# Gated linear attention and a 4-bit MLP on one core: other home counts, the key factors behind the chunk's step, and identity matmuls at the start

## The chip, the cores and the metric

The kernel runs on one core of one Trainium2 chip. The metric is the device time of the whole program in microseconds (us); the time before is the median of three runs. TensorE is called PE, its weight loads PEld, VectorE DVE, ScalarE ACT, GpSimd POOL and SyncE, which issues nearly all transfers, SP.

## The reference

Two residual blocks follow each other, on x of 4 batches x 512 tokens x 512 features, all in 32-bit floats:

```python
x = x + attention(layernorm(x))        # 4 heads of 128, chunks of 128 tokens
x = x + mlp(layernorm(x))              # 512 -> 4096 -> 512
```

The attention is gated and linear. From the normed x come q, k, v (512 wide each), and for each head a gate alpha = sigmoid(...) and a weight beta = softplus(...). k is divided by its norm over each head. In each chunk, with cla the running sum of log(alpha):

```python
attn   = (q @ k.T) * beta.T * tril(exp(cla - cla.T))
y      = attn @ v + exp(cla) * (q @ state)
state  = state * exp(cla_end) + v.T @ (k * beta * exp(cla_end - cla))
```

The MLP's weights come as 4-bit codes, two to a byte in an integer, with a scale for each block of 32:

```python
inter = gelu_tanh(x @ Wg.T) * (x @ Wu.T)     # 2048 tokens x 4096
out   = inter @ Wd.T
```

## The kernel before

**Stages.** The attention phase fills about the first 300 us, the MLP overlaps its last 70 us and runs to the end. Attention goes over 4 batches b; each batch has twelve steps, counted through by p: j = 0 to 3 make v and the gates' inputs for one tile of 128 tokens (`product_v`, PE lines 381 and 388), j = 4 to 7 make one head of q (`product_q`, L406), j = 8 to 11 one tile of k (`product_k`, L418). After each step stands `behind(p)`, which adds what lies behind that product: for the chunk number (p - 9) // 3 it is, in turn for p % 3 = 0, 1, 2, the lead (k transposed at L520, copied by ACT to kT at L523), the values (kw and vb, POOL L569 and L573) and the decay (ACT's exponentials L536, POOL's causal mask L540, qc and the state's decay); then the scores (PE L581, DVE L589); then the sums (PE L600 to L611, DVE adds y to the residual tile xr at L616, stores it at L617, starts the second layernorm, and updates the state at L620 or L622).

**Norms.** A layernorm has three parts. `norm` issues statistics (DVE L310, L312, POOL L314, L315); `settle` writes the normed tile hn (DVE L320); `turn("a")` (first norm) or `turn("f")` (second) transposes it on PE (L341) and copies it out: for the first norm ACT writes hT (L351), for the second ACT and DVE split it into three parts g (L362 to L364), which SP stores to DRAM (h2, L366). For the MLP they are loaded again as x (L296), twelve tiles of 128x512 for a batch.

**MLP.** A round i takes one batch (i % 4) through up to four blocks of 128 of the 4096 columns. For each block `gate_up` makes two products (pa eight matmuls, pb four, L696), with the elementwise work at L701 to L718; each product's value stands in a tile called t. `down` then multiplies into eight PSUM banks (p_d, L734) and adds to the accumulator tiles acc (DVE L747 and L748), which are stored (L749) and loaded again four rounds later. There are 35 rounds. The x tiles of the next round are loaded in two parts: the first six during this round, the rest after this round's last product (`load_x`). The 4-bit weights are unpacked by DVE and ACT one piece at a time (`unpack`, `fetch`), ahead of their use.

**Order.** The whole order of each engine is written out by hand: the program is issued in source order under a manual schedule, each engine works through its own list, and semaphores hold an instruction back until its inputs are there and its buffers are free.

**Homes.** Nearly all on-chip tiles live in slots called homes, of 4 KB a partition (`two_k`) or 2 KB (`one_k`). The free ones are a list: `get` takes the home that was given back longest ago, `put` appends. When no small home is free, `get` takes a large one whole. A new tile in a home waits for the last reader of the tile that was in it before, a store to DRAM among them. PSUM has eight banks, handed round in turn.

**The start.** SP issues the loads in order, ACT issues four small ones (Wab, bab, bv, bq) and then an exponential on a dummy value (`warm`, which loads the table). `first(n)` is norm and settle of tile n; the copy of Wab into the joint weight tile is POOL's L833. During batch 0 `product_v` calls `between` between its two products: turn("a"), and the norm of the tile after next.

Of the kernel before, what the change touches and what calls it, by code (L numbers as in the profile page):

```python
# [21 lines left out]
P = 128  # L22
# [13 lines left out]
def f32(t):  # L36
    return t.bitcast(F32)
# [3 lines left out]
def tile_gated_linear_attention__then__nvfp4_geglu(  # L41
# [19 lines left out]
    nc = tc.nc  # L61
    B, T, D = x.shape
    H = D // P
    NCH = T // P
# [52 lines left out]
                else:  # L117
                    self.free.append(tag)

    two_k = Homes("a", 24, [P, 2, T])  # L120
    one_k = Homes("b", 42, [P, T], two_k)

    def psum(name):
        return fps.tile([P, T], F32, tag="p", name=name)

    def heads(t):
        return t.rearrange("p (h d) -> p h d", d=P)
# [5 lines left out]
    ident = const.tile([P, P], F32, tag="ident", name="ident")  # L133
# [160 lines left out]
    def load(src, name):  # L294
        t = one_k.get(name)
        nc.sync.dma_start(f32(t), src)  # L296
        return t

    def tile_of(t):
        return xf[t * P : (t + 1) * P, :]  # L300

    def rows(src, c):
        return src.rearrange("(c p two) n -> c p two n", p=P, two=2)[c]
# [26 lines left out]
    def settle():  # L330
        for then in settled:
            then()
        settled.clear()
# [80 lines left out]
    def product_k(b, n):  # L414

        pk = psum(f"pk_{b}_{n}")
        for k in range(KC):
            nc.tensor.matmul(  # L418
                pk, f32(hT[b][k // 2])[:, k % 2, n * P : (n + 1) * P], f32(wk[k // 2])[:, k % 2, :],
                start=(k == 0), stop=(k == KC - 1),  # L420
            )
        kt = one_k.get(f"k_{b}_{n}")
        k_sb[b, n] = kt
        nc.vector.tensor_tensor(f32(kt), pk, f32(bk_sb), ALU.add)
        sq = one_k.get(f"sq_{b}_{n}")
        nc.scalar.activation(f32(sq), f32(kt), AF.Square)
        sn = small.tile([P, H], F32, tag="ss", name=f"ss{b}_{n}")
        nc.vector.tensor_reduce(sn, heads(f32(sq)), AX.X, ALU.add)
        one_k.put(sq)
        nc.gpsimd.tensor_scalar(sn, sn, 1e-24, None, ALU.max)  # L430
        nc.gpsimd.tensor_tensor(sn, sn, minus_half, ALU.pow)
        brn = small.tile([P, H], F32, tag="brn", name=f"brn{b}_{n}")
        nc.gpsimd.tensor_tensor(brn, sn, beta[b][:, n * H : (n + 1) * H], ALU.mult)
        kwf = small.tile([P, H], F32, tag="kwf", name=f"kwf{b}_{n}")
        nc.gpsimd.tensor_tensor(kwf, sn, bdte[b][:, n * H : (n + 1) * H], ALU.mult)
        ss[b, n] = brn, kwf
# [189 lines left out]
    for b in range(1, B):  # L626
        for n in range(NCH):
            p = 3 * NCH * (b - 1) + 3 * n - 1 if b > 1 else 2 + 3 * min(n, 2)
# [50 lines left out]
    jk = [(j, k) for j in range(3) for k in range(KC)]  # L679
    x3 = [[] for _ in rounds]  # L680

    def load_x(i, which):
        if i < len(rounds):
            for j, k in which:
                x3[i].append(load(h2d[i % B][j][k], f"x_{i}_{j}_{k}"))
# [73 lines left out]
    def mlp():  # L759
        for i, r in enumerate(rounds):  # L760
            ts = range(i % B * NCH, (i % B + 1) * NCH)
            ms = tiles[i]
            inter = []
            a4 = residual(i) if i > 1 else None
            ahead = [0] if i >= B - 1 else [i] if i > 0 else []
            for q, mt in enumerate(ms):
                if q in ahead:
                    load_x(i + 1, jk[:6])

                def last():  # L770

                    if q == len(ms) - 1:
                        one_k.put(*x3[i])
                        if i == 1:
                            nonlocal a4
                            a4 = residual(i)
                        load_x(i + 1, jk[len(x3[i + 1]) :] if i + 1 < len(rounds) else [])

                inter.append((yield from gate_up(mt, x3[i], 2 if i == 1 else 1, r + MC, last, f"{i}_{mt}", mt == ms[-1] and len(ms) < 3)))
                if mt == r and mt < tiles[-1][0]:  # L780
                    two_k.put(*wgu[mt])
            final = i + B >= len(rounds)
            dst = [of[t * P : (t + 1) * P, :] if final else accd[t] for t in ts]
            if i == 0:
                over = ms, inter
                continue
            if i == B:
                ms, inter = over[0] + ms, over[1] + inter
            down(ms, inter, a4, dst, f"{i}", i == len(rounds) - 1)
            if r >= 0 and r % 2 == 1 and r < tiles[-1][0]:  # L790
                two_k.put(*wd[r // 2])
            yield


    with tc.manual_schedule():
        wab_sb = const.tile([P, KC, 2 * H], F32, tag="wab", name="wab_sb")
        bq_sb = const.tile([P, H], F32, tag="bq", name="bq_sb")
        bab_sb = const.tile([P, 2 * H], F32, tag="bab", name="bab_sb")
        bv_sb, bk_sb = one_k.get("bv"), one_k.get("bk")
        wva = [two_k.get(f"wva{c}") for c in range(KC // 2)]  # L800
        wvb = two_k.get("wvb")
        wvb_ = f32(wvb).rearrange("p two (k n) -> p (two k) n", n=VB + 2 * H)
        wq, wk = ([two_k.get(f"w{nm}{c}") for c in range(KC // 2)] for nm in "qk")
        x0 = [load(tile_of(0), "x0_0")]
        nc.scalar.dma_start(
            wab_sb.rearrange("p (c two) n -> p c two n", two=2),
            Wab.rearrange("(c p two) n -> p c two n", p=P, two=2),
        )
        nc.scalar.dma_start(bab_sb, bab.partition_broadcast(P))
        nc.scalar.dma_start(f32(bv_sb), bv.partition_broadcast(P))  # L810
        nc.scalar.dma_start(bq_sb, bqT)

        warm = small.tile([P, 1], F32, tag="warm", name="warm")
        nc.scalar.activation(warm, eps_la, AF.Exp)
        for c in range(KC // 2):
            nc.sync.dma_start(f32(wva[c])[:, :, :VA], rows(Wv, c)[:, :, :VA])
        x0.append(load(tile_of(1), "x0_1"))
        for c in range(KC // 2):
            nc.sync.dma_start(wvb_[:, 2 * c : 2 * c + 2, :VB], rows(Wv, c)[:, :, VA:])
        x0 += [load(tile_of(n), f"x0_{n}") for n in range(2, NCH)]  # L820
        for w, src in ((wq, Wq), (wk, Wk)):
            for c in range(KC // 2):
                nc.sync.dma_start(f32(w[c]), rows(src, c))
        nc.sync.dma_start(f32(bk_sb), bk.partition_broadcast(P))
        for n in range(NCH):
            xs[1, n] = load(tile_of(NCH + n), f"x1_{n}")

        def first(n):
            first_norm(0, n, x0[n])
            settle()  # L830

        first(0)
        nc.gpsimd.tensor_copy(wvb_[:, :, VB:], wab_sb)  # L833
        constants()
        turn("a")
        first(1)
        blocks = mlp()
        p = 0
        for b in range(B):
            for j in range(3 * NCH):  # L840
                if j < NCH:
                    if b == 0:

                        def between():
                            turn("a")
                            if j + 2 < NCH:
                                first(j + 2)

                        product_v(b, j, between)
                    else:  # L850
                        product_v(b, j)
                elif j < 2 * NCH:
                    product_q(b, j - NCH)
                else:
                    product_k(b, j - 2 * NCH)
                if b == B - 1:
                    if j == NCH - 1:
                        two_k.put(*wva, wvb)
                        one_k.put(bv_sb)
                    elif j == 2 * NCH - 1:  # L860
                        two_k.put(*wq)
                    elif j == 3 * NCH - 1:
                        two_k.put(*wk)
                        one_k.put(bk_sb)
                if j == 3 * NCH - 1:
                    two_k.put(*hT[b])
                behind(p)
                if p in (5, 7):
                    fetch()
                if p > 3 * NCH and p % 3:  # L870
                    unpack(1, MT)
                p += 1
                if b == B - 1 and j == 2 * NCH - 3:
                    load_x(0, jk)
                if b == B - 1 and j == 2 * NCH + 1:
                    for _ in range(2):
                        next(blocks)
                        behind(p)
                        p += 1
        for _ in blocks:  # L880
            behind(p)
            p += 1
# [48 lines left out]
```

## Time and profile before

| what | us |
|---|---|
| median of 3 runs (1324.4 to 1329.06) | 1324.96 |
| profiled execution | 1324.66 |
| its span | 1322.9 |
| PE busy in the span | 1301.6 |
| DVE busy | 975.4 |
| ACT busy | 441.8 |
| POOL busy | 123.7 |

The span is what the profiler saw between the first and the last instruction; 1.76 us of the profiled execution lie around it. The mean granted clock of PE is 0.997 of full speed. The costliest groups of instructions are PE's: pa (L696) 508.5 us in 2048 matmuls of 390 ns, p_d (L734) 356.8 us in 1536 of 390 ns and pb (L696) 275.8 us in 1024; then DVE's L702 with 176.6 us. The transfers move 236.57 MB at a mean of 179 GB/s, 420 loads of x among them, of 256 KB each. In a row of a timeline stand the start, the duration, engine, line, operation, the tile written and the tiles read, the number of instructions drawn together, and in brackets the idle time of the engine ahead of it and what ended it. In a table of windows, each engine's busy time and its instructions are followed by the granted clock, the share of the DMA engines that was busy, and GB/s.

### The profile page before, as it was taken

Reading aid. Unit: us, or ns where it says so; the run is one execution under the profiler, and the core shown is the slowest. Engines: PE = TensorE matmul, PEld = TensorE weight load, DVE = VectorE, ACT = ScalarE, POOL = GpSimd, SP = SyncE. Lnnn points to the kernel's source line nnn. Section 1 sums busy time; section 2 is a strip of 40 time slices with the busy share of each in tenths; the row PEclk is TensorE's granted clock in tenths of the full one; section 3 lists DMA queues with packets and bytes.
Section 4 is the critical chain, followed back from the end, with each engine's and each line's share of the span. In section 5 each row is a group of like instructions: output and inputs, shape, how many; then the busy total and the mean of one; then the engine's idle time right before and its main releaser. Section 6 shows DMA issues by size and latency. Waiting matters only on the chain.

```text
span 1322.9 us, 16906 instructions
## 1 busy us (share of the span) xinstructions
PE 1301.6 (98%) x5800; PEld 1040.2 (79%) x5800; DVE 975.4 (74%) x1533; ACT 441.8 (33%) x777; POOL 123.7 (9%) x220
## 2 busy tenths in 40 slices
PE   7999999989999999999999999999999999999998
PEld 5676676677888888888888888888888888887886
DVE  3477776687767777777777777787878787877566
ACT  1333324453333333333333333333333333332332
POOL 1445453420000000000000000000000000000000
PEclk9999999989999999999999999999999999999999
DMA  7033346578546565655565656564656565555463
GB/s 239 9 96 112 117 123 199 187 259 270 186 153 197 170 203 179 192 178 194 174 203 167 203 173 203 163 219 160 209 160 211 169 201 168 199 175 184 167 241 141
DMA packets 173798, 236.57 MB, mean 179 GB/s; under 512 B 15760, under 2 KB 74128, under 8 KB 173712
## 3 DMA queue, kind: packets, MB, share of 16 engines
q1 hardware_dynamic: 173008, 235.20, 54.5%
q8 instruction: 46, 0.75, 0.2%
q10 hardware_dynamic: 704, 0.28, 0.1%
q14 instruction: 40, 0.33, 0.1%
HBM read 183.00 MB, written 52.43 MB: 178 GB/s over the span
## 4 chain that ended last, share of the span: by engine, by line
PE 93%; DVE 3%; DMA 2%; POOL 1%; issue 1%; ACT 1%; SPq 0%; DVEq 0%; ACTq 0%; POOLq 0%
PE pa L696 34%; PE p_d L734 25%; PE pb L696 17%; PE pq L406 4%; PE pk L418 3%; PE pva L381 2%; PE pvb L388 2%; DMA x<-h 1%; PE sp L581 1%; PE yp L609 1%; PE yp L611 1%; PE dp L600 1%; PE tp_a L341 1%; PE tp_f L341 0%; PE tpk L520 0%
## 5 line engine op out<-in xcount | busy, mean ns | idle before, releaser
L696 PE MATMUL pa<-x,wgu 128*128 128x512 f32 x2048 | 508.5, 390 | 0.2 <-DMA x<-h 0.2
L696 PEld LDWEIGHTS pa<-x,wgu 128*128 128x128 f32 x2048 | 384.9, 188 | 80.6 <-DMA x<-h 0.9
L734 PE MATMUL p_d<-wd,i 128*128 128x512 f32 x1536 | 356.8, 390 | 1.8 <-DVE state L622 0.8
L734 PEld LDWEIGHTS p_d<-wd,i 128*128 128x128 f32 x1536 | 287.7, 188 | 65.1 <-DVE i L718 1.6
L696 PE MATMUL pb<-x,wgu 128*128 128x512 f32 x1024 | 275.8, 390 | 1.1 <-DMA x<-h 0.4
L701 ACT ACTIVATE t<-pb 128x512 f32<-128x512 f32 x256 | 151.3, 591 | 349.2 <-PE pb L696 346.5
L702 DVE TENSOR_TENSOR t<-pa,t 128x512 f32<-128x512 f32 x256 | 176.6, 690 | 95.4 <-ACT t L701 90.1
L696 PEld LDWEIGHTS pb<-x,wgu 128*128 128x128 f32 x1024 | 192.2, 188 | 43.6 <-DMA x<-h 3.5
L747 DVE SCALAR_TENSOR_TENSOR acc<-p_d,acc 128x512 f32<-128x512 f32 x136 | 93.3, 686 | 109.1 <-PE p_d L734 109.1
L714 ACT ACTIVATE i<-t 128x512 fp32r<-128x512 f32 x128 | 81.0, 633 | 198.2 <-DVE t L711 195.1
L706 ACT ACTIVATE t<-t 128x512 f32<-128x512 f32 x128 | 81.1, 634 | 154.3 <-DVE t L702 154.2
L717 DVE TENSOR_TENSOR i<-t,i 128x512 fp32r<-128x512 f32 x128 | 88.2, 689 | 25.9 <-ACT i L714 22.7
L748 DVE TENSOR_TENSOR acc<-acc,p_d 128x512 f32<-128x512 f32 x136 | 93.6, 689 | 14.2
L711 DVE SCALAR_TENSOR_TENSOR t<-t,t 128x512 f32<-128x512 f32 x128 | 88.7, 693 | 4.4
L718 DVE SCALAR_TENSOR_TENSOR i<-i,t 128x512 fp32r<-128x512 f32 x128 | 87.7, 685 | 0.1
L418 PE MATMUL pk<-wk,hT 128*128 128x512 f32 x128 | 57.4, 592 | 0.0
L406 PE MATMUL pq<-hT,wq 128*128 128x512 f32 x128 | 57.2, 592 | 0.0
L406 PEld LDWEIGHTS pq<-hT,wq 128*128 128x128 f32 x128 | 23.8, 190 | 24.2 <-issue 23.7
L418 PEld LDWEIGHTS pk<-wk,hT 128*128 128x128 f32 x128 | 23.5, 190 | 23.6 <-issue 23.4
L188 DVE SCALAR_TENSOR_TENSOR w_gu<-i_gu,sc_gu 128x1024 f32<-128x1024 f16 x32 | 40.1, 1253 | 0.0
L200 DVE TENSOR_TENSOR wgu<-wgu,wgu 128x1024 fp32r<-128x1024 f32 x32 | 39.0, 1219 | 0.0
L197 DVE SCALAR_TENSOR_TENSOR wgu<-wgu,w_gu 128x1024 fp32r<-128x1024 f32 x32 | 38.9, 1216 | 0.0
(121 smaller groups left out, 892.9 us busy)
## 6 DMA issues: line engine op xcount, KB each, us to landing
x<-h SPq DMA_DIRECT2D x420, 256.0 KB
acc<-acc SPq DMA_DIRECT2D x256, 256.0 KB
h<-g SPq DMA_DIRECT2D x48, 256.0 KB
x<-in_x SPq DMA_DIRECT2D x16, 256.0 KB
pk_gu<-in_gate_p SPq DMA_DIRECT2D x32, 128.0 KB
sc_gu<-in_gate_s SPq DMA_DIRECT2D x64, 64.0 KB
pk_gu<-in_up_p SPq DMA_DIRECT2D x32, 128.0 KB
sc_gu<-in_up_s SPq DMA_DIRECT2D x64, 64.0 KB
```

The source lines that it names most:

```text
L406: nc.tensor.matmul(pq, f32(wq[k // 2])[:, k % 2, h * P : (h + 1) * P], f32(hT[b][k // 2])[:, k % 2, :], start=(k == 0), stop=(k == KC - 1),)
L418: nc.tensor.matmul(pk, f32(hT[b][k // 2])[:, k % 2, n * P : (n + 1) * P], f32(wk[k // 2])[:, k % 2, :], start=(k == 0), stop=(k == KC - 1),)
L696: nc.tensor.matmul(o, w3[j][:, k % 2, c * P : (c + 1) * P], x[j * KC + k], start=(j == js[0] and k == 0), stop=(j == js[-1] and k == KC - 1),)
L701: nc.scalar.activation(f32(t), pb, AF.Copy, scale=-1.0 / ONE_E)
L702: nc.vector.tensor_tensor(f32(t), pa, f32(t), ALU.add)
L706: nc.scalar.activation(f32(g), f32(g), AF.Gelu_apprx_tanh, scale=ONE_E)
L711: nc.vector.scalar_tensor_tensor(f32(u), f32(g), ONE_E, f32(u), ALU.mult, ALU.mult)
L717: nc.vector.tensor_tensor(il, f32(u), f32(ih), ALU.subtract)
L718: nc.vector.scalar_tensor_tensor(im, f32(ih), ONE_E, f32(u), ALU.mult, ALU.subtract)
L734: nc.tensor.matmul(o, inter[i][j][:, n * P : (n + 1) * P], wd[ms[i] // 2][j][:, ms[i] % 2, :], start=(i == 0 and j == js[0]), stop=(i == L ...
L747: nc.vector.scalar_tensor_tensor(a, pas[2 * n], ONE_E, a, ALU.mult, ALU.add)
L748: nc.vector.tensor_tensor(a, a, pas[2 * n + 1], ALU.subtract)
```

## The change

Four things are different.

1. The homes: 27 large and 36 small ones in place of 24 and 42.
2. `product_k` ends with the addition of the bias. Its second half, the Square on ACT (L426), the reduction on DVE (L428) and the four small POOL operations that make the factors brn and kwf, is a function of its own, which is issued behind the `behind(p)` of the same step.
3. In round 1 the first part of the load of the next x is three tiles instead of six; the other nine then follow in the second part.
4. At the start SP loads x0_0 and x0_1 first, ACT's four small loads are issued by SP between the others, and PE begins with twelve matmuls of the identity with itself, into a bank that nothing reads. `product_v` of the fourth tile of batch 0 gets no `between`, so that the transposes of the second batch's first tile come a step later, in `behind(4)`.

```diff
-    two_k = Homes("a", 24, [P, 2, T])
-    one_k = Homes("b", 42, [P, T], two_k)
+    two_k = Homes("a", 27, [P, 2, T])
+    one_k = Homes("b", 36, [P, T], two_k)
...
         nc.vector.tensor_tensor(f32(kt), pk, f32(bk_sb), ALU.add)
+        return lambda: k_factors(b, n, kt)
+
+    def k_factors(b, n, kt):
         sq = one_k.get(f"sq_{b}_{n}")
         nc.scalar.activation(f32(sq), f32(kt), AF.Square)
...
-                    load_x(i + 1, jk[:6])
+                    load_x(i + 1, jk[: 6 if i > 1 else 3])
...
-        x0 = [load(tile_of(0), "x0_0")]
-        nc.scalar.dma_start(
-            wab_sb.rearrange("p (c two) n -> p c two n", two=2),
-            Wab.rearrange("(c p two) n -> p c two n", p=P, two=2),
-        )
-        nc.scalar.dma_start(bab_sb, bab.partition_broadcast(P))
-        nc.scalar.dma_start(f32(bv_sb), bv.partition_broadcast(P))
-        nc.scalar.dma_start(bq_sb, bqT)
+        x0 = [load(tile_of(n), f"x0_{n}") for n in range(2)]
+
+        busy = psum("busy")
+        for i in range(12):
+            nc.tensor.matmul(busy[:, :P], ident, ident, start=True, stop=True)
...
         for c in range(KC // 2):
             nc.sync.dma_start(f32(wva[c])[:, :, :VA], rows(Wv, c)[:, :, :VA])
-        x0.append(load(tile_of(1), "x0_1"))
+        nc.sync.dma_start(
+            wab_sb.rearrange("p (c two) n -> p c two n", two=2),
+            Wab.rearrange("(c p two) n -> p c two n", p=P, two=2),
+        )
+        nc.sync.dma_start(f32(bv_sb), bv.partition_broadcast(P))
         for c in range(KC // 2):
             nc.sync.dma_start(wvb_[:, 2 * c : 2 * c + 2, :VB], rows(Wv, c)[:, :, VA:])
+        nc.sync.dma_start(bab_sb, bab.partition_broadcast(P))
         x0 += [load(tile_of(n), f"x0_{n}") for n in range(2, NCH)]
+        nc.sync.dma_start(bq_sb, bqT)
...
+                later = None
...
-                        product_v(b, j, between)
+                        product_v(b, j, between if j + 1 < NCH else None)
...
-                    product_k(b, j - 2 * NCH)
+                    later = product_k(b, j - 2 * NCH)
...
                 behind(p)
+                if later:
+                    later()
```

## The prediction

> **What bounds the kernel now.** I read the page's busy rows and slices first, then the windows, then the timeline where the windows show holes.
>
> ```profile
> PE 1301.6 (98%) x5800; PEld 1040.2 (79%) x5800; DVE 975.4 (74%) x1533; ACT 441.8 (33%) x777; POOL 123.7 (9%) x220
> PE   7999999989999999999999999999999999999998
> PEclk9999999989999999999999999999999999999999
> PE 93%; DVE 3%; DMA 2%; POOL 1%; issue 1%; ACT 1%; SPq 0%; DVEq 0%; ACTq 0%; POOLq 0%
> ```
>
> TensorE is busy for 1301.6 of 1322.9 us, and 93% of the chain that ended last is its own work. The change takes no matmul away, so it can win at most the 21.3 us in which PE idles, and the time in which PE is busy at a slow clock. Two slices are thin, the first and the ninth (264 to 298 us). The windows say where the holes are:
>
> ```profile
> 0.00:12.00 12.00, 5.53 (x18) 4.17 (x19) 4.67 (x13) 2.18 (x5) 3.29 (x18) 1.00 0.84 264
> 245.00:260.00 15.00, 12.87 (x65) 8.77 (x64) 10.53 (x17) 7.59 (x14) 9.71 (x14) 1.00 0.89 301
> 260.00:280.00 20.00, 16.49 (x82) 14.05 (x80) 14.40 (x21) 9.61 (x16) 6.39 (x10) 0.83 0.62 186
> 330.00:363.00 33.00, 33.00 (x147) 27.35 (x146) 26.14 (x39) 10.60 (x18) 0.00 (x0) 1.00 0.58 183
> ```
>
> Columns after the length: busy PE, PEld, DVE, ACT, POOL, then clock, DMA share, GB/s. PE idles 6.5 us before 12, 2.1 in 245 to 260, 3.5 in 260 to 280. From 330 on it is never idle (33.00 of 33; 926.4 of 927 in 363 to 1290), with DVE at 0.76 and DMA at 0.57. **So the start and the hand-over from attention to MLP can gain, and the steady rounds can only lose.**
>
> **The start.** TensorE's timeline:
>
> ```profile
> 6.01 1.11 PE L341 MATMUL tp_a<-ident,hn_a 128*128 128x128 f32 x4 [6.01 <-DVE hn_a L320]
> 7.58 3.88 PE L381 MATMUL pva<-wva,hT 128*128 128x264 f32 x8 [0.46 <-ACT hT L351]
> 13.48 1.94 PE L381 MATMUL pva<-wva,hT 128*128 128x264 f32 x8
> 24.57 0.63 PE L341 MATMUL tp_a<-ident,hn_a 128*128 128x128 f32 x4 [1.25 <-DVE hn_a L320]
> ```
>
> The first x lands at 3.49, its norm ends at 5.96, and until then PE has nothing. The first product then takes 3.88 us where the next of its shape takes 1.94, and the first transposes 1.11 where later ones take 0.60 to 0.66: a slow clock (the page's clock row has no record for it here). *Identity matmuls.* Twelve of them are 24 records of 128x128. The nearest rows are the scores' eight of that size: 1.05 to 1.16 us at full clock, 2.07 at the slow one, so 0.13 or 0.26 each. ident is ready at 1.46 (POOL), so they begin near 1.5 and sit ahead of the first transpose in PE's queue. By the trace PE needed from 6.01 to 11.46, 5.4 us, to become fast: 20 records slow (5.2), 4 fast (0.5), an end at 7.3, 1.3 us past hn_a. The Trainium skill ("TensorE: Matmul & The Clock Gate", Part 1, the clock gate) says that about 3.4 us of sustained work release the clock, in a window that runs freely: 13 slow (3.4), 11 fast (1.4), an end at 6.3, 0.3 past hn_a. Its Part 4 says that transposes count otherwise than matmuls; leaving them out, the trace's own figure is 3.88, near the rule, so I take the rule. Either way transposes and product come out fast: 1.11 - 0.62 + 3.88 - 1.94 = 2.4 gained, less 0.3 (2.1), or less 1.3 (1.1).
> *Loads.* x0_1 was issued at 2.59 and landed at 8.31; it moves ahead of two 264 KB loads. ACT's four loads go to SP, about 0.45 us of issue each (1.8 in all), ahead of which the wva loads stand. The second block of PE, tp_a at 11.26, follows the first directly, so PE will then wait for the second norm: before, 8.31 + 2.5 (statistics to hn_a, 8.31 to 10.77) = 10.8. With x0_1 landing near 5, that cover exists. It fails if wab, now behind wva, holds the copy at POOL's L833 (5.33 before), and behind it the second norm's rs: wab would have to land after about 7.5 to matter.
> *The block moved.* The gap of 1.25 at 23.3 is tp_a of the second batch waiting for its norm; it now stands behind a q product (4 x 0.592 = 2.4 us), so it goes. Start: 2.1 + 1.25 = **3.3 gained** (bounds 1.0, if loads hold the second norm, and 4.0). PE is full from 26 to 245 but for three gaps under 0.4, so it is carried.
>
> **Square and factors.** Two stalls stand in the hand-over:
>
> ```profile
> 248.67 0.69 DVE L424 TENSOR_TENSOR k<-pk,bk 128x512 f32<-128x512 f32 x1
> 249.39 0.63 ACT L426 ACTIVATE sq<-k 128x512 f32<-128x512 f32 x1 [6.11 <-DVE k L424]
> 249.93 0.57 ACT L523 COPY kT<-tpk 128x512 f32<-128x512 f32 x1
> 250.55 1.16 PE L581 MATMUL sp<-q,kT 128*128 128x128 f32 x8 [1.74 <-ACT kT L523]
> ...
> 267.51 0.63 ACT L714 ACTIVATE i<-t 128x512 fp32r<-128x512 f32 x1 [5.15 <-DVE t L711]
> 268.04 0.57 ACT L523 COPY kT<-tpk 128x512 f32<-128x512 f32 x1
> 268.66 2.07 PE L581 MATMUL sp<-q,kT 128*128 128x128 f32 x8 [3.51 <-ACT kT L523]
> ...
> 271.24 3.45 PE L696 MATMUL pa<-x,wgu 128*128 128x512 f32 x8
> ```
>
> First stall: tpk ended at 245.1, but the copy of kT stood on ACT behind a Square that waited for DVE's k. With the Square behind the step, kT is done near 245.8 and the 1.74 goes. ACT had been idle for 6.11, so nothing else is late on it. The factors are seven instructions a chunk (Square 0.63, reduce 0.69, four small POOL operations, 2.7 together in the 257 us row), and they come later by what the step puts on DVE, 3 us at most; the first to need them is vb on POOL, and PE needs that a step or two later (2.4 us each with pk): hidden. In return dm, kw and vb no longer stand behind them: dm's multiplication (L589) was at 255.24 and waited 0.56 for POOL; it comes near 252. The stores of g and the loads of x behind them come 1.2 us earlier, which takes about 0.9 of 1.3 us from the pb at 253.88 (2.40 us instead of 1.07, four waits for x).
> Second stall: kT at 268.04 stands behind L714, which waited 5.15 for DVE, whose chain starts with xr at 262.06. That chain comes about 2.5 us earlier, PE about 2.7; I see 1.3 of the 3.5 going. The clock fell to 0.74 and 0.58 here: 2.07 against 1.05, 1.06 against 0.60, 3.45 against 2.02, together 2.9 us. The skill's same page ("Why this matters for your kernels") warns of idle gaps over 3 us; with 2.2 left, the rule keeps the clock and the row (a drop at 3.5) does not contradict it. Gross: 1.7 + 0.9 + 1.3 + 2.9 = **6.8**.
>
> **Homes.** The bytes are the same, 24 x 4 + 42 x 2 = 27 x 4 + 36 x 2 = 180 KB a partition. But a small home is handed out again sooner, and the next writer waits for its last reader. Following the lists through, t1 of the second gate_up gets the home of a g whose store to h2 takes 3.4 us from issue to landing (240.68 to 244.13 for such a store), so ACT's L701 comes no earlier than before, near 275.5; other tiles of that stage wait for stores of acc (about 1.5 us on the ACT-DVE chain near 290). Behind L701 stand the DVE steps that free the bank for p_d (L622), which already waited 0.78. These give back between 0 and all 6.8, and up to 1.5 more; nearest to a row is the first, at the old time exactly, so that the gain ahead of it becomes a wait there. The earlier loads of x_2, three instead of six, move 0.77 MB to a later burst: 1.4 us later, with the down between. I keep **1.3 of the 6.8** (bounds -1.5 and 6.8).
> Steady rounds: I count 33 to 36 small homes live at the peak, out of 36, and large ones serve in need. The second half of a round's x loads now waits for the round's last pa. Six loads of 0.61 issue and some 2 us of landing make 6; the down hides 10.9 and the first four columns more. Zero, unless the slack goes.
>
> **Sum.** The profiled execution is 1324.66 us (span 1322.9 and 1.76 around it), 0.3 under the median of 1324.96. 1324.66 - 3.3 - 1.3 = 1320.1, so **1320**.
>
> **Rivals.** A difference under 0.5%, 6.6 us, cannot be told from none here.
> A, forecast: the start carried, the hand-over nearly neutral: 1317 to 1323. Chance 0.50; some of it falls under 1318.3.
> B: the hand-over keeps its gain: 1324.66 - 3.3 - 6.8 = 1314.6. For it speaks that most of the 6.8 is one clock drop, which goes whole or not at all; against, the home of t1. Chance 0.27.
> C, slower: the small homes, with none free, bind in the steady rounds. It decides once a wait outlasts the 10.9 us of the down: with acc stores, dequantisation loads and x loads in one burst, the first pb waits as at 314.6 to 319.7, where such a pair took 5.09 instead of 2.72. A seventh of that, 0.3 us, in each of 32 rounds is +10, 1331; the whole 2.4 would be far beyond. For it: 36 of 36. Against: DMA at 0.57, and idle zero today. Chance 0.15.
> D: the burst runs over its cover and the norms wait for SP's longer queue, so the start gives nothing; the hand-over neutral: 1324. Chance 0.08.
>
> **Range.** 1313 to 1331 takes in B's best and C's usual price. Faster by over 0.5% is B and about a fifth of A, 0.38; slower is C with the rest of its tail, 0.15; within, 0.47.
>
> **What would show it.** Right: a first pva near 2 us right behind busy matmuls that end by 6.5; no gap near 22; no idle before the sp near 245; a clock of 1.00 in 255 to 280; p_d near 280 waiting longer than 0.78. Wrong: busy matmuls to 7.5 or later, tp_a of x0_1 waiting; the clock still dropping near 265 (A's lower end); pb or pa waiting for x in any window after 330 (C); PE below 33.00 of 33 there.

## The result and the profile after

The changed kernel takes 1323.36 us (median of 20 runs), the kernel before 1325.18 (20 runs): a ratio of 0.9985, 95% interval 0.9978 to 0.9992. That is 1.8 us of the 5 forecast (1324.96 less 1320). The profiled execution took 1323.24 us, its span is 1321.5.

First the page of the changed kernel, busy rows and PE's slices, then the windows that were shown of before. (Columns as there.)

```profile
PE 1304.4 (99%) x5824; PEld 1044.4 (79%) x5824; DVE 973.6 (74%) x1533; ACT 434.8 (33%) x777; POOL 126.9 (10%) x220
PE   9999999889999999999999999999999999999998
```

```profile
0.00:12.00 12.00, 9.93 (x49) 8.88 (x50) 4.66 (x13) 2.78 (x6) 3.45 (x18) 1.00 0.78 238
245.00:260.00 15.00, 12.67 (x70) 10.08 (x68) 10.79 (x17) 5.17 (x7) 8.51 (x14) 1.00 0.64 204
260.00:280.00 20.00, 14.38 (x64) 11.42 (x65) 12.66 (x20) 8.12 (x14) 5.26 (x8) 0.81 0.64 192
330.00:363.00 33.00, 33.00 (x148) 27.31 (x147) 26.66 (x41) 11.29 (x18) 0.00 (x0) 1.00 0.57 190
```

PE's 99% is no sign of a gain: the first window is now full of identity matmuls. The hole in 260 to 280 has grown from 3.5 to 5.6 us, and the clock there is as low as it was. The steady rounds are as full as before. On ACT, though, something has changed. Its largest waits for t between 345 and 1300 us, before and after (total, times, longest), ended with PE's product and now end with stores of acc tiles, whose homes t gets:

```profile
ACT t L701 <- PE pb L696: 329.8, 62, 13.6
ACT t L704 <- DMA acc<-acc: 281.1, 26, 13.5
```

With the smaller entries, ACT's waits for t come to 330.5 us before and 339.3 after; PE feels nothing of it.

What decided can be read off one table: the start of the same PE instruction in both traces, and how far the changed kernel is ahead.

| PE instruction | before, us | after, us | ahead, us |
|---|---|---|---|
| tpk, batch 1 | 124.32 | 121.37 | 2.95 |
| sp ahead of the first stall | 235.22 | 230.57 | 4.65 |
| sp at the first stall | 250.55 | 244.00 | 6.55 |
| tpk ahead of the second stall | 261.56 | 254.22 | 7.34 |
| sp at the second stall | 268.66 | 262.19 | 6.47 |
| first p_d | 278.04 | 270.57 | 7.47 |
| tpk behind that down | 285.00 | 283.28 | 1.72 |
| third down | 338.78 | 336.65 | 2.13 |
| end of the span | 1322.9 | 1321.5 | 1.4 |

So the change wins 7.5 us up to 270, gives back 5.75 in the first down, and 0.7 in the 985 us from the third down to the end.

**The start after.** PE's timeline of the changed kernel:

```profile
1.52 5.17 PE L811 MATMUL busy<-ident 128*128 128x128 f32 x24 [1.52 <-POOL ident masks.py:199]
6.53 0.60 PE L341 MATMUL tp_a<-ident,hn_a 128*128 128x128 f32 x4
7.59 2.05 PE L381 MATMUL pva<-wva,hT 128*128 128x264 f32 x8 [0.46 <-ACT hT L351]
9.72 0.66 PE L341 MATMUL tp_a<-ident,hn_a 128*128 128x128 f32 x4
```

The identity matmuls hold the first transposes until 6.53, but transposes and product are fast at once (0.60 for 1.11, 2.05 for 3.88). The product still begins at 7.59, as before at 7.58: what is won is won inside it and behind it.

**The hand-over after.** All engines, the rows that carry the loss:

```profile
249.20 0.69 DVE L363 TENSOR_TENSOR g<-tp_f,g 128x512 fp32r<-128x512 f32 x1 [2.71 <-DMA acc<-xr]
...
261.03 0.63 ACT L717 ACTIVATE i<-t 128x512 fp32r<-128x512 f32 x1 [6.02 <-DVE t L714]
261.57 0.57 ACT L526 COPY kT<-tpk 128x512 f32<-128x512 f32 x1
...
262.19 2.07 PE L584 MATMUL sp<-q,kT 128*128 128x128 f32 x8 [4.37 <-ACT kT L526]
...
271.80 0.60 ACT L704 ACTIVATE t<-pb 128x512 f32<-128x512 f32 x1 [3.81 <-DMA h<-g]
272.43 0.69 DVE L705 TENSOR_TENSOR t<-pa,t 128x512 f32<-128x512 f32 x1 [3.12 <-ACT t L704]
...
275.82 0.68 DVE L619 TENSOR_TENSOR xr<-xr,yp 128x512 f32<-128x512 f32 x1
...
276.55 1.22 PE L737 MATMUL p_d<-wd,i 128*128 128x512 f32 x2 [2.87 <-DVE xr L619]
```

Read it from the bottom. p_d waits 2.87 us for a bank that DVE's addition to xr frees; that addition stands behind t's chain on DVE (272.43 to 275.8); t waits for ACT; and ACT waits 3.81 us for a transfer that has nothing to do with t, a store of g, because t got g's home. In the same way DVE's L363 waits 2.71 us for a store of xr, and behind it the whole chain to kT, so that the second stall is 4.37 us instead of 3.51. Releasers of the kind "DMA h<-g" or "DMA acc<-xr" ahead of an instruction that reads neither are how a reused buffer looks in a profile.

The waits are only half of what the first down costs. From the first p_d to the tpk behind it PE took 6.96 us before (278.04 to 285.00) and 12.71 after (270.57 to 283.28). Of the 5.75 more, 2.7 are idle time (3.44 against 0.78); the other 3.1 are matmuls that ran longer. These are the last thirteen of the 24 p_d, before and after, and two windows of the changed kernel (third number from the right: the granted clock):

```profile
281.91 3.25 PE L734 MATMUL p_d<-wd,i 128*128 128x512 f32 x13 [0.78 <-DVE state L622]
278.07 5.37 PE L737 MATMUL p_d<-wd,i 128*128 128x512 f32 x13 [0.30 <-DVE state L625]
```

```profile
275.87:279.28 3.41, 2.43 (x5) 1.52 (x6) 2.90 (x6) 0.00 (x0) 1.67 (x3) 0.50 1.01 311
279.28:282.69 3.41, 3.41 (x10) 2.64 (x9) 3.15 (x6) 0.00 (x0) 0.15 (x1) 0.50 1.03 384
```

Behind the wait for the bank the clock fell a second time, to half, for 6.8 us.

### The profile page after: what moved, and what is told of

Read it like the earlier page. It is cut to its first block, busy times and chain, and to the rows that moved or that the text cites. A ratio compares the mean times of both kernels' runs of the same rounds, so it can differ in the third digit from the quotient of the medians.

```text
span 1321.5 us, 17008 instructions
## 1 busy us (share of the span) xinstructions
PE 1304.4 (99%) x5824; PEld 1044.4 (79%) x5824; DVE 973.6 (74%) x1533; ACT 434.8 (33%) x777; POOL 126.9 (10%) x220
## 4 chain that ended last, share of the span: by engine, by line
PE 91%; DVE 4%; ACT 2%; DMA 2%; issue 1%; SPq 0%; POOL 0%; POOLq 0%; ACTq 0%; DVEq 0%
PE pa L699 32%; PE p_d L737 25%; PE pb L699 16%; PE pk L418 4%; PE pq L406 4%; PE pva L381 2%; PE pvb L388 2%; PE sp L584 1%; PE yp L612 1%; DVE t L705 1%; PE dp L603 1%; PE yp L614 1%; ACT t L704 1%; DVE t L714 1%; DMA h<-g 1%
```

## Experiments

Theory: the start and the factors win what they should, and the smaller number of small homes takes most of it away. Each ratio is to the kernel before on the same chip, with its 95% interval.

**e1: the old numbers of homes.**

```diff
-    two_k = Homes("a", 27, [P, 2, T])
-    one_k = Homes("b", 36, [P, T], two_k)
+    two_k = Homes("a", 24, [P, 2, T])
+    one_k = Homes("b", 42, [P, T], two_k)
```

> The changed kernel with 24 large and 36+6 small homes again, all else as changed. Theory (homes): in the changed kernel PE is 7.4 us ahead at the first p_d and 5.7 of that is lost there, because t of the second block's second product (ACT L704) waits 3.8 us for a store of g that had its home; with the old counts that wait is gone, the idle time at p_d falls from 3.4 us to under 1, and the time is 1318 to 1320. Rival (DVE chain): p_d waits for its PSUM bank behind a DVE chain that is late whatever the homes; then the idle at p_d stays near 3 and the time is 1323 to 1324.

1318.85 us, 0.9952 (0.9939 to 0.9964): 4.5 us faster than the changed kernel. The same rows in its timeline:

```profile
261.01 1.16 PE L584 MATMUL sp<-q,kT 128*128 128x128 f32 x8 [2.47 <-ACT kT L526]
...
266.71 0.59 ACT L704 ACTIVATE t<-pb 128x512 f32<-128x512 f32 x1
...
272.10 0.73 PE L737 MATMUL p_d<-wd,i 128*128 128x512 f32 x2 [2.01 <-DVE xr L619]
...
273.62 4.83 PE L737 MATMUL p_d<-wd,i 128*128 128x512 f32 x13 [0.78 <-DVE state L625]
```

ACT's t waits for nothing, the second stall is 2.47, sp runs at the full clock (1.16), and it is 10.25 us ahead of before at the first p_d. The idle at p_d did not fall under 1, though: 2.0 and 0.8 stay, so DVE's chain is a bound there by itself, as the rival had it, but 4 us earlier. And the clock, kept at sp, falls here: the thirteen matmuls take 4.83 us against 3.25 before.

**e2: the start alone**, put into the kernel before (identity matmuls, order of loads, the moved block).

> The kernel before with the new start alone (order of loads, identity matmuls, the moved block). Theory: the lead of 2.95 us that the two traces show at 30 us is carried to the end, since all engines of the hand-over shift with it: 1322.2, with stalls of 1.7 and 3.5 us before the scores as before. Rival: the hand-over is timed by something that doesn't shift (transfers), and eats it: 1324 to 1325.

1321.82 us, 0.9972 (0.9961 to 0.9983): 3.6 us, carried to the end.

**e3: the factors alone**, put into the kernel before (the diff of `product_k` and the two lines behind `behind(p)`).

> The kernel before with the Square and the factors behind the chunk's step alone. Theory: the small gaps at 128 to 192 us (0.9) and the first stall (1.7) go, the pb of the first block gains 0.7, the second stall grows by 0.9 and the clock drop after it shrinks by 1; with the old homes p_d loses little, so 1321 to 1322.5. Rival (DVE chain): what is won before 260 us comes back as a wait at p_d even with the old homes: 1324 to 1325.

1321.27 us, 0.9971 (0.9959 to 0.9982): 4.1 us faster. With the old homes it is kept. The second stall did not grow, as the theory had it, but fell from 3.51 to 2.50 us; the clock fell behind it all the same (sp took 2.07 us).

**e4: the homes alone**, put into the kernel before.

> The kernel before with 27 large and 36 small homes alone, six and six x tiles as before. Theory (homes): t of the second block's second product waits for the store of g, p_d waits longer: 1326 to 1329. Rival: the wait is hidden, since that t was no earlier than 275.7 us before either: 1324.5 to 1325.5. Steady rounds (third possibility): PE idles in windows after 330 us, above 1330.

1331.55 us, 1.0050 (1.0037 to 1.0062): 6.2 us slower, more than the theory said, and as much as the third possibility. Its place, though, is not the steady rounds. PE's longest waits in e4 between 225 and 345 us (total, times, longest); before, the same list has 5.2 at sp, so no loss there, and a single 0.8 at p_d:

```profile
PE sp L581 <- ACT kT L523: 5.0, 2, 4.3
PE p_d L734 <- DVE xr L616: 2.8, 1, 2.8
PE p_d L734 <- ACT t L701: 1.2, 1, 1.2
```

At the first p_d e4 is level with before (277.84 against 278.04), at the tpk behind it 6.5 us late (291.48 against 285.00), and at the second down still 6.5 (312.75 against 306.23). The first down took 13.64 us against 6.96: 3.6 more of idle time, and 3.1 of slow matmuls as in the changed kernel (thirteen in 5.39 us).

**e5: one tile moved to a large home**, the t that waits 3.8 us, in the changed kernel (`get` has a second argument, which asks for a large home).

```diff
-            t = one_k.get(f"t{i}_{key}")
+            t = one_k.get(f"t{i}_{key}", (i, key) == (1, "1_1"))
```

> The changed kernel, 27 and 36 homes kept, with one tile moved: t of round 1's second block, second product, takes a large home. Every engine's order is unchanged. Theory (two home waits): its wait of 3.8 us for the store of g goes, t is ready near 268.7 instead of 272.4, the idle at p_d falls from 3.4 to about 1 to 2.8 as in e1, and the second stall stays at 4.4: 1320 to 1321.5. Rival: the next wait in line takes its place (bank of p_d behind xr's addition), and the time stays at 1323 to 1324.

1324.04 us, 0.9990 (0.9984 to 0.9997): nothing won, as the rival said. Yet the wait did cost time where it stood: the first down is 5.2 us shorter than in the changed kernel, 2.0 of it idle time and the rest the clock, which now stays (the thirteen matmuls take 3.25 us again). It is lost behind it. **e6: g1 and g2 of the last batch's first chunk as well.**

> As e5, and g1 and g2 of the first chunk of the last batch take large homes too, so that DVE's L363 no longer waits 2.7 us for the store of xr whose home it got. Theory: the second stall falls from 4.4 to about 2.5 as in e1, with no clock drop; with e5's part this is the whole cost of the homes: 1318 to 1319.5. Rival: the second stall of e1 was shorter because the dequantisation steps stood elsewhere in DVE's list with the old counts, not because of g; then it stays over 4 and the time is that of e5.

1322.25 us, 0.9975 (0.9967 to 0.9983): about a quarter of the 4.5. The second stall fell to 2.46 as in e1, so it was g's wait that made it long, not the order of DVE's list as the rival said. But the timeline shows the next in line:

```profile
260.38 2.08 PE L584 MATMUL sp<-q,kT 128*128 128x128 f32 x8 [2.46 <-ACT kT L526]
...
285.40 0.60 ACT L704 ACTIVATE t<-pb 128x512 f32<-128x512 f32 x1 [5.15 <-DMA acc<-acc]
...
288.51 0.49 PE L612 MATMUL yp<-vb,dm 128*128 128x128 f32 x2 [1.78 <-DVE dm L592]
```

A later t waits 5.15 us for a store of acc, DVE's list behind it is late, and PE waits 1.78 for the masked scores (in e5 1.77). **e9: this t in a large home too.**

> As e6, and the first t of round 2 takes a large home too, whose wait of 5.2 us for a store of acc stood ahead of the last chunk's scores in e6. Theory (a row of home waits, each hiding the next): ACT's wait at 285 us and PE's idle of 1.8 us ahead of yp there go, 1320 to 1321. Rival: what keeps e6 from e1's 1318.9 is later loads of x, whose homes also wait for stores; then the time stays at 1321.8 to 1322.6.

1320.04 us, 0.9962 (0.9949 to 0.9974): yp's wait is gone from PE's list. How far PE is ahead of the changed kernel, at three places:

| kernel | tpk behind the first down | second down | third down | median, us |
|---|---|---|---|---|
| e5, one tile | 5.4 | 0.5 | 0.2 | 1324.04 |
| e6, and g1, g2 | 7.2 | 2.2 | 0.3 | 1322.25 |
| e9, and the next t | 7.2 | 4.6 | 4.0 | 1320.04 |
| e1, old homes | 5.0 | 4.0 | 3.7 | 1318.85 |

Each repair wins what it should up to the next hole, and loses it there. For e5 and e6 that is above all the later t. What e6 loses between the second and the third down is not a wait for a home: PE waits 1.4 us there for tiles of x, and then the clock falls to half, which it doesn't in e9:

```profile
315.00:318.40 3.40, 3.35 (x7) 2.44 (x8) 0.00 (x0) 0.59 (x1) 0.00 (x0) 0.50 1.04 396
315.00:318.40 3.40, 3.40 (x17) 2.82 (x16) 2.10 (x3) 1.72 (x3) 0.00 (x0) 1.00 0.97 334
```

So the homes' cost is a row of waits, each hiding the next, with drops of the clock behind some of them. These four tiles account for 3.3 of 4.5 us by the medians. A rest is not shown: the intervals of e9 and e1 overlap, and the two profiled executions have the same span, 1317.1 us.

**e10: 25 and 40.**

> The changed kernel with 25 large and 40 small homes (27 and 36 as changed, 24 and 42 in e1). Theory: the fewer small homes, the sooner one is handed out again; with 40 the two waits for stores at 246 and 268 us are gone and others stay, 1319 to 1321. Rival: the waits depend on which home happens to come next and not on the count; then anything from 1317 to 1325.

1318.81 us, 0.9954 (0.9942 to 0.9967): no slower than 24 and 42. So it isn't graded evenly: the cost comes between 40 and 36. That it depends on which home happens to come next, and not on the count, is not ruled out: the rival's range takes this result in too.

**e7: no identity matmuls**, the loop of twelve taken out of the changed kernel.

> The changed kernel without the twelve identity matmuls, all else as changed. Theory: the first transposes take 1.1 and the first product 3.9 us again (together 2.3 more than at the full clock), less 0.5 in which the identity matmuls kept the transposes waiting; the lead shrinks by 1.8 to 2.3 at 30 us. Carried to the end: 1325 to 1325.6. Rival: the tail of the hand-over, which waits for stores and DVE, absorbs it: 1323.4 to 1324.

1325.72 us, 1.0000 (0.9992 to 1.0008). PE's timeline at its start:

```profile
6.04 1.12 PE L341 MATMUL tp_a<-ident,hn_a 128*128 128x128 f32 x4 [6.04 <-DVE hn_a L320]
7.61 3.88 PE L381 MATMUL pva<-wva,hT 128*128 128x264 f32 x8 [0.46 <-ACT hT L351]
11.29 1.06 PE L341 MATMUL tp_a<-ident,hn_a 128*128 128x128 f32 x4
25.50 1.88 PE L406 MATMUL pq<-hT,wq 128*128 128x512 f32 x4
```

The first q product begins at 25.50; with the identity matmuls it begins at 23.78. These 1.7 us are most of the 2.4 between the medians. The matmuls that compute nothing are worth more than the net of the whole change.

**e11: start and factors with old homes, six and six. e12: the changed kernel with six and six.**

> Start and factors as changed, homes 24 and 42, six and six x tiles: e2 and e3 together. Theory: the two parts add up, -3.6 and -4.1, so 1317.5 to 1318; the split of three and nine then costs about 1 in e1. Rival: the split does nothing with the old homes: 1318.5 to 1319.2.

> The changed kernel with six and six x tiles again. Theory: three and nine belong to the smaller number of homes, since three tiles more would hold homes through the second block; without it 1324 to 1326, so that the split gives back some of what the homes cost. Rival: the split costs here what it costs with the old homes, about 1: 1322 to 1322.8.

e11: 1317.23 us, 0.9947 (0.9934 to 0.9959), which is e2 and e3 added (-3.6 and -4.1). e12: 1324.33 us, 0.9995 (0.9986 to 1.0005). With the old homes three and nine is 1.6 us slower by the medians, with the new ones 1.0 faster; in both pairs the intervals overlap, so neither is more than a hint that the split belongs to the smaller number. e11 and e12 differ in the homes alone, by 7.1 us; the changed kernel and e1 by 4.5, e4 and the kernel before by 6.2.

**e8: the copy of kT earlier**, on top of e11. Next to the MLP the lead of the next chunk (`pending` holds its `chunk_lead`) is issued from inside `gate_up`:

```diff
         u = product(1)
+        if pending:
+            pending.pop()()
         last()
```

> Start and factors as changed, homes 24 and 42, six and six x tiles, and one move more: next to the MLP the transposes of k and their copy to kT (ACT L526) are issued ahead of a block's L717 instead of behind it, so the copy no longer waits for DVE's t. Theory: the second stall (2.5 us in e1) goes, but hn for tp_f comes at 258.3 at the earliest and p_d waits for DVE's xr (2.0 us in e1), which isn't moved, so part comes back: 1316.5 to 1318.5. Rival: DVE bounds the whole stage and all comes back at p_d: 1318.5 to 1319.5.

1317.26 us, 0.9937 (0.9925 to 0.9950). Inside the range of the theory, but it is e11 and not e1 that it has to be held against, and e11 has 1317.23: the move wins nothing that the medians show. PE's waits of e8 from 225 to 345 us say where it went:

```profile
PE p_d L747 <- DVE xr L619: 2.2, 1, 2.2
PE yp L612 <- DVE dm L592: 1.9, 1, 1.9
```

sp begins at 257.34 instead of 260.21, and the stall ahead of it is gone; but yp now waits 1.9 us and p_d waits as long as in e11 (2.0). Of 2.9 us 0.8 are left at the first p_d. As the rival said, DVE bounds the stage. e11 and e8 are the fastest of all kernels here, 8 us under the kernel before: the change without its homes.

## Why the prediction held, and where it did not

The direction held, and the median of 1323.4 lies inside 1313 to 1331, but 0.4 above the end of case A (1317 to 1323), and 1.8 us were won where 5 were forecast. That it lies inside owes more to the width of the range than to the working: the start's term held, and the term for the hand-over had the wrong sign. Of the signs of being right, the fast first product (behind matmuls that ended at 6.7, not 6.5), no gap near 22, no idle time ahead of the sp near 245 and the longer wait at p_d came; the clock of 1.00 from 255 to 280 did not, and its fall near 265 stood among the signs of being wrong. By the steps:

- **Start, 3.3.** The traces show 2.95 at 120 us and e2 3.6 at the end. The identity matmuls kept the first transposes until 6.53, 0.5 us later than before. The end at 6.3 that was worked out from the Trainium skill ("TensorE: Matmul & The Clock Gate", Part 1) is nearer to that than the 7.3 from the trace's first product, but that is partly luck. The estimate counted its 3.4 us from the first matmul; in the trace the 24 records start 0.21 us apart up to the 22nd and 0.11 to 0.14 from there, so the clock came at about 6.2, 4.7 us after the first, and in other runs with the same start the 24 took 4.28 us (e6) and 5.49 (e1). The price stayed small because a slow record took 0.21 us, not the 0.26 reckoned. The fear for wab came near: POOL's copy waited 1.50 us for it and ran at 7.12, under the 7.5 named.
- **Factors, first stall, 1.7, and pb, 0.9.** The stall is gone, pb takes 1.76 instead of 2.40 (0.64). Not counted at all: the small gaps at 128 to 192 us, which I listed as harmless; they and what surrounds them gave 1.7 more (2.95 to 4.65 ahead).
- **Second stall, 1.3, and the clock, 2.9.** Wrong for the kernel as changed: the stall grew by 0.86, and the clock fell. The stall was about right for the step taken by itself: 2.50 in e3 and 2.47 in e1 (forecast 2.2). What failed there was the separation of this step from the homes: I followed the lists to t of the second block, and to the acc stores near 290, but not to g1, whose wait for xr's store stands in the same DVE chain. The clock failed with the old homes too. That a stall under 3 us keeps it was taken as a rule; in e3 it fell behind 2.50 us, and in e1 it held at sp and fell at p_d. So the 2.9, the largest single term of the 6.8 (though not "most" of it), was not there to be won whole.
- **Homes: "I keep 1.3 of the 6.8".** The mechanism, the tile (ACT's t behind the store of g) and the place (p_d waiting longer than 0.78) are those that the traces show; t came only 3.7 us ahead of the time named (271.80 against 275.5), with PE 7.5 ahead. The size is wrong, and the term that was left out is the clock behind that wait: 3.1 of the 5.75 us lost in the first down are slow matmuls, for which the sum had nothing. Without the homes the change is worth 7.9 us (e11), with them 1.8: they take about 6 us, the same as alone (6.2 in e4). The hand-over therefore stands at some -1.8 (1.8 less the start's 3.6), just past its lower bound of -1.5, not at +1.3. I reckoned the loss as a gain that is eaten; e4 shows it as a cost of its own, which is there when nothing is won ahead of it.
- **Steady rounds, zero.** 33.00 of 33 in the window, and 0.7 us more in 985. The time of rival C did not come: e4's price is its 6 us, but paid once, in the hand-over. Waits for stores of acc did come, but on ACT, where PE doesn't feel them (281.1 us; with 40 small homes, in e10, 0.9).
- **Rival B** (1314.6, the hand-over keeping its 6.8): nearest to it are the kernels with the old homes, e11 and e8, at 1317.2; the factors are worth 4.1 there.
- **What can be told from none.** The prediction put that at 6.6 us; here 1.8 us are enough, since the interval of the ratio ends at 0.9992.

## What to carry to other kernels

When buffers are handed out in turn, their number sets how soon one comes back, and a tile stored to DRAM holds its buffer until the store has landed: look in the waits for transfers ahead of instructions that don't read what they moved. One such wait repaired may show nothing in the time (e5), because the next stands behind it; that is no proof against the cause, and the lead at fixed instructions along the trace shows it where the median does not. Reckon a wait on PE with the clock behind it: here 3.4 us of waits in one down brought 3.1 us of slow matmuls. Test each part of a change alone: here two parts worth 3.6 and 4.1 us, which add up, were hidden under a third that cost 6.

## What was not expected of the hardware

A stall of one length took the clock in some kernels and left it in others. PE was idle for 2.47 us ahead of sp in e1 and for 2.46 in e6; the same eight matmuls of sp then took 1.16 and 2.08 us. There e10 (2.6) and e11 (2.5) kept the clock, e9 (2.4) and e3 (2.5) lost it. So in this kernel idle time of some 2.5 us is not safe, and its length alone doesn't decide.

The traces hold more. In all fourteen the granted clock changes only on a grid: in the changed kernel it was full for 256.00 us, half for 3.41, full for 10.24, half for 6.83, which is 75, 1, 3 and 2 times 3.413 us, and where the grid lies against the program differs from trace to trace (the clock of the first matmuls came at 4.4 us in e6, at 7.5 in e1). Here are the stretches of that grid around the stall, first of e1, then of e6 (columns as before; the first number behind the length is PE's busy time):

```profile
256.71:260.12 3.41, 1.84 (x8) 1.16 (x7) 3.02 (x4) 0.26 (x1) 2.51 (x3) 1.00 0.77 253
260.12:263.53 3.41, 2.52 (x17) 2.35 (x18) 2.58 (x4) 3.38 (x8) 0.04 (x1) 1.00 0.00 1
```

```profile
256.95:260.36 3.41, 0.97 (x5) 0.47 (x3) 3.38 (x5) 1.12 (x3) 1.69 (x2) 1.00 0.31 82
260.36:263.77 3.41, 3.39 (x14) 3.29 (x15) 1.77 (x3) 3.39 (x7) 0.92 (x2) 0.50 0.38 109
```

In e1 the stall is split over two stretches, 1.57 us of idle time in one and 0.89 in the next; in e6 it lies in one, 2.44, and the next stretch runs at half the clock. Others fit:

| stretch at full clock | idle in it, us | clock in the next |
|---|---|---|
| e11, 255.77, ahead of sp | 1.48 | 1.00 |
| e10, 256.03, ahead of sp | 1.55 | 1.00 |
| e7, 258.37, ahead of sp | 1.82 | 1.00 |
| e8, 269.42, at p_d | 1.98 | 0.50 |
| changed kernel, 272.45, at p_d | 2.18 | 0.50 |
| before, 263.95, ahead of sp | 2.20 | 0.50 |
| e1, 270.36, at p_d | 2.53 | 0.50 |

From 13 to 310 us, in all fourteen traces, eighteen stretches lost the clock, each with at least 1.98 us of idle time, and none with 1.82 or less did. At p_d of e1 two waits, of 2.0 and 0.8 us, fall almost whole into one stretch and add up. This is read from traces; no run moved a stall along the grid to test it. And it isn't the whole: near 315 us, where x comes tile by tile, e2, e3, e6 and e12 lost the clock behind stretches with 1.1 to 1.3 us of idle time. The Trainium skill ("TensorE: Matmul & The Clock Gate", Part 1) has a window of about 3.4 us that runs freely, and the grid agrees with it; the idle time of a whole window that it names is more than was enough here.
